# Attention probabilities turned in 32x32 squares on VectorE and weighed on four 32-row quarters of TensorE, in a layernorm, attention and low-rank feed-forward layer

## The chip, the core and the metric

The kernel runs on one core of one Trainium2 chip. The metric is device time in microseconds. A core has TensorE (PE: matmuls, with its weight loads shown apart as PEld), VectorE (DVE), ScalarE (ACT), GpSimd (POOL) and SyncE (SP, which issues most of the DMAs). SBUF has 128 partitions; a matmul result goes to one of eight PSUM banks, each of 512 floats a partition.

## The reference

All arrays are float32. `x` is 4 x 512 x 1024; there are 32 query heads, 8 key heads (so 4 query heads share a key head), and a head has 128 values.

```python
xn = layernorm(x)
qkv = xn @ w_qkv                        # 1024 x 6144
q, k, v = split(qkv)                    # 32 query heads, 8 key heads, 8 value heads
scores = einsum('bqhgd,bkhd->bhgqk', q, k) * scale
bias = -slope[h, g] * sqrt(q_pos - k_pos), and -inf where the key is later than the query
attn = softmax(scores + bias)
out = einsum('bhgqk,bkhd->bqhgd', attn, v) @ w_o
ffn = xn @ W.T + b + (one of four low-rank products, chosen for each token by a gate)
return x + out + ffn
```

## The kernel before

Three stages follow one another. `project` normalises the tokens, turns them, and multiplies them by `w_qkv`; queries, keys and values go to DRAM. `attend` computes the attention for 32 units one after another: a unit is one pair of batches `p`, one key head `h` and one batch `bi` of the pair. `finish` multiplies the heads by `w_o` and the tokens by `W` in one long product. Both big products are done in the manner of Strassen and Winograd, two levels deep: operands are summed beforehand on DVE and POOL, seven products replace eight, and the results are summed afterwards. That is why `attend` also forms sums of its results (`outer_sums`, `outer_steps`, `middle_sums`) and stores them for `finish`, on DVE and POOL beside its own work.

In `project`, an `item` is one such product. When a quarter of its result is complete, `after` (L593) has `put` (L584) store it, some steps later (`in_while`): keys and values of two heads each in one tile `t`, 128 partitions (the 128 values of a head) by 2 heads by 512 tokens (L591). The steps are numbered by `pace[2]`, and `beside` runs what has become due.

In `attend`, a tile of scores has 128 rows: 32 queries of each of four heads, so that partitions 32g to 32g+31 hold head `g` (`C` is 32, `G` is 4, `R` is 4). A unit has 16 such tiles, in four groups `i` = 3, 2, 1, 0 of four. Since a query sees no later key, tile `j` = 4i + r has only (j + 1) x 32 columns. `scores` (L1024) does one matmul for each tile (L1033), adds the distances and finds the least value on DVE (L1038), takes the exponential with its sum on ACT (L1042), and scales the rows by the inverted sum on POOL (L1047). What a tile doesn't compute in the last 128 columns of its group was cleared once (L1173).

To weigh the values, keys must lie on partitions. `transpose_probs` (L1053) turns squares of 128 by 128 on PE with an identity (L1058), four into one bank, and copies the bank to SBUF, on DVE or ACT in turn (L1061, L1063). `weigh` (L1066) then multiplies: for group `i` there are i + 1 matmuls of 512 columns, with 128 keys of the values as weights and the four heads' queries as columns (L1071), and ACT copies the bank into the result `O`, in order of heads (L1072). A unit has 40 such transposes, and ten matmuls in `weigh`. `values` (L1016) turns the unit's values on PE beforehand, four transposes and a copy, from the tile `vT`, which `load` (L984) brings with `q` and `k` two units ahead.

PE's and SP's instructions run in the order in which the code issues them (`manual_schedule`); on the other engines the tile framework orders them. The loop at L1180 mixes two units: while unit `u` is turned and weighed, the scores of the next one, `nxt`, are computed. For each `i`: `scores(nxt, i)`, then pieces of the sums (`aside`), `weigh` of a group turned two steps earlier, `transpose_probs(u, i)`. PSUM's banks are shared out by `rotation` (L1162): three for scores, three for transposes, two for results. Beside the last unit, `fill` puts in the first products of `finish`.

Of the kernel before, what the change touches and what calls it, by code (L numbers as in the profile page):

```python
# [21 lines left out]
P = 128  # L22
NH, NKV, D = 32, 8, 128
G = NH // NKV
# [41 lines left out]
def kernel(  # L66
# [55 lines left out]
    um_d = [scratch(f"um{i}", [RMAX + 1, S]) for i in range(B)]  # L122
    q_d = {(i, h): scratch(f"q{i}_{h}", [P, S // C, G, C]) for i in range(B) for h in range(NKV)}
    k_d = {(i, h): scratch(f"k{i}_{h}", [P, 2, S]) for i in range(B) for h in range(0, NKV, 2)}
    v_d = {(i, h): scratch(f"v{i}_{h}", [P, 2, S]) for i in range(B) for h in range(0, NKV, 2)}
    s_d = {i: scratch(f"s{i}", [P, 7, NP, 2, KB, HS]) for i in OUTER}
    t_d = scratch("t", [P, 4, 2, 2, 2 * KB, HS])
    m_d = {i: scratch(f"m{i}", [P, 4, 2 * KB, HS]) for i in OUTER}
# [235 lines left out]
    def project(attention):  # L364
# [5 lines left out]
        with pool("a") as sb, tc.tile_pool(name="stats", bufs=2, reuse_waits="tile") as stats:  # L370
# [182 lines left out]
            def item(st, i, acc):  # L553
# [30 lines left out]
                def put(t, row, col):  # L584
                    bi = 2 * p + row
                    if kind == "q":
                        src = t.rearrange("p a b -> p (a b)").rearrange("p (j f) -> p j f", f=2 * C)
                        dst = q_d[bi, h].rearrange("p j g k -> p j (g k)")
                        nc.sync.dma_start(out=dst[:, :, ts(col, 2 * C)], in_=src)
                    else:  # L590
                        nc.sync.dma_start(out=(k_d, v_d)[col][bi, h], in_=t)  # L591

                def after(row, col):  # L593
                    left[0] -= 1
# [365 lines left out]
    def attend(front, begin):  # L960


        early = pool("bq", side="right")
        with ExitStack() as stack:
            sb, sq = None, early.__enter__()
            units = [(p, h, bi) for p in range(NP) for h in range(NKV) for bi in range(2)]
            sizes = {"dist": (S,), "q": (S // C, G, C), "k": (S,), "vT": (S,), "bias": (S,)}
            counts = {"q": 2, "k": 2, "vT": 2, "v": 2, "pt": 10, "o": 4, "ot": 2}
            for i in (3, 2, 1, 0):
                for b in range(2):  # L970
                    sizes[f"p{i}{'xy'[b]}"] = (R, (i + 1) * P)
            sizes.update(v=(NT, D), pt=(S,), os=(3, 2, S), o=(G, S), ot=(9, HS))
            queries = ("dist", "q", "k", "vT", "bias")

            def buf(tag, name):
                where = sq if tag in queries else sb
                return where.tile([P, *sizes[tag]], F32, tag=tag, name=name, bufs=counts.get(tag, 1))

            Q, K, VT, V, PR, O, bias = {}, {}, {}, {}, {}, {}, {}

            def label(u):
                return "_".join(str(k) for k in u)
# [1 line left out]
            def load(u, queue=nc.sync):  # L984
                p, h, bi = u
                n = label(u)
                K[u] = buf("k", f"k_{n}")
                Q[u] = buf("q", f"q_{n}")
                VT[u] = buf("vT", f"vT_{n}")
                queue.dma_start(out=K[u], in_=k_d[2 * p + bi, h - h % 2][:, h % 2])  # L990
                queue.dma_start(out=Q[u], in_=q_d[2 * p + bi, h])
                queue.dma_start(out=VT[u], in_=v_d[2 * p + bi, h - h % 2][:, h % 2])

# [18 lines left out]
                bias[p, h] = t  # L1014

            def values(u):  # L1016
                n = label(u)
                V[u] = buf("v", f"v_{n}")
                tr = bank("tr", f"v_{n}")
                for t in range(NT):  # L1020
                    nc.tensor.transpose(tr[:, ts(t, P)], VT[u][:, ts(t, P)], ident)
                nc.scalar.copy(V[u], tr.rearrange("p (t d) -> p t d", d=D))

            def scores(u, i):  # L1024
                p, h, bi = u
                m = f"{label(u)}_{i}"
                tot = sb.tile([P, R], F32, tag=f"tot{i}", name=f"tot_{m}", bufs=2)
                pr = PR[u, i] = probs[i, units.index(u) % 2]
                rows = [pr[:, r, : (R * i + r + 1) * C] for r in range(R)]
                for r, row in enumerate(rows):  # L1030
                    n = (R * i + r + 1) * C
                    sc = bank("sc", f"{m}_{r}")
                    nc.tensor.matmul(  # L1033
                        sc[:, :n], Q[u][:, n // C - 1].rearrange("p g k -> p (g k)"), K[u][:, :n], start=True, stop=True
                    )

                    low = sb.tile([P, 1], F32, tag=f"low{r}", name=f"low_{m}_{r}", bufs=2)
                    nc.vector.tensor_tensor_reduce(  # L1038
                        row, sc[:, :n], bias[p, h][:, S - n :], -SCALE, BIG,
                        ALU.add, ALU.min, low,  # L1040
                    )
                    nc.scalar.activation(  # L1042
                        row, row, AF.Exp, bias=low, scale=-1.0, accum_out=tot[:, r : r + 1]
                    )
                nc.vector.reciprocal(tot, tot)  # L1045
                for r, row in enumerate(rows):
                    nc.gpsimd.tensor_scalar(  # L1047
                        row, row, tot[:, r : r + 1], 1.0, ALU.mult, ALU.mult
                    )

            PT, OS = {}, {}

            def transpose_probs(u, i):  # L1053
                for j in range(i + 1):
                    m = f"{label(u)}_{i}_{j}"
                    tr = bank("tr", m)
                    for r in range(R):
                        nc.tensor.transpose(tr[:, ts(r, P)], PR[u, i][:, r, ts(j, P)], ident)  # L1058
                    pt = buf("pt", f"pt_{m}")
                    if j % 2 == 0:  # L1060
                        nc.vector.tensor_copy(pt, tr)  # L1061
                    else:
                        nc.scalar.copy(pt, tr)  # L1063
                    PT[i, j] = pt

            def weigh(u, i):  # L1066
                if u not in O:
                    O[u] = buf("o", f"o_{label(u)}")
                po = bank("o", f"{label(u)}_{i}")
                for j in range(i + 1):  # L1070
                    nc.tensor.matmul(po, V[u][:, j, :], PT[i, j], start=(j == 0), stop=(j == i))  # L1071
                nc.scalar.copy(  # L1072
                    O[u][:, :, ts(i, P)].rearrange("p g (r k) -> p g r k", k=C),
                    po.rearrange("p (r g k) -> p g r k", r=R, k=C),
                )

            last = (NP - 1, NKV - 1)

# [80 lines left out]
            distances(units[0])  # L1159
            yield  # L1160
            sb = stack.enter_context(pool("b"))
            bank = rotation(sc=(0, 1, 2), tr=(3, 6, 7), o=(4, 5))  # L1162

            for tag in "ot os o".split():
                buf(tag, f"lay_{tag}")

            probs = {
                (i, b): buf(f"p{i}{'xy'[b]}", f"p_{i}_{b}") for i in (3, 2, 1, 0) for b in range(2)
            }
            for b in range(2):  # L1170
                for i in (3, 2, 1, 0):
                    for r in range(R - 1):
                        nc.gpsimd.memset(probs[i, b][:, r, (R * i + r + 1) * C :], 0.0)  # L1173
            for tag in "v pt".split():
                buf(tag, f"lay_{tag}")
            for i in (3, 2, 1, 0):
                scores(units[0], i)
                if i == 3:
                    values(units[0])
            for n, u in enumerate(units):  # L1180
                p, h, bi = u
                nxt = units[n + 1] if n + 1 < len(units) else None
# [3 lines left out]
                if n == len(units) - 6:  # L1186
                    front[0]()
                if not nxt:
                    early.__exit__(None, None, None)
                    front[1](O[p, h, 0])  # L1190
                    fill = begin()
                if bi == 1:
                    beside.append(middle_sums(p, h, (1, 2), "o", O[p, h, 0], True))
                for i in (3, 2, 1, 0):
                    if nxt:
                        scores(nxt, i)
                    if i > 1:
                        aside(outer, 1)
                    aside(below, 2)
                    if i < 2 or not nxt and i < 3 or n == close - 2 and i == 2:  # L1200
                        aside(beside, 2)
                    if i < 2:
                        weigh(u, i + 2)
                        if i == 0 and not nxt:
                            outer_sums(p, h, slice(HS, S))
                        next(fill, None)
                    transpose_probs(u, i)
                    next(fill, None)
                    if i == 2 and nxt:
                        values(nxt)  # L1210
                    if i == 3:
                        aside(outer, 1)
                    if not nxt:
                        if i == 3:
                            aside(beside, 2)
                        if i == 2:
                            while beside:
                                aside(beside, 1)
                        if i < 2:
                            front[3 - i]()  # L1220
                if after and after[2] == 0:
                    distances(after)
                aside(beside, 2)
                weigh(u, 1)
                next(fill, None)
                weigh(u, 0)
                if n == close:

                    while beside:
# [533 lines left out]
```

## Time and profile before

| | us |
|---|---|
| median of 3 runs | 2612.72 (2612.28 to 2616.37) |
| profiled execution, its own time | 2614.29 |
| its span, first to last instruction | 2612.5 |
| PE busy | 2559.6 (98%) |
| DVE busy | 1774.3 (68%) |
| ACT busy | 608.5 (23%) |
| POOL busy | 1911.8 (73%) |

A matmul call in float32 appears as two pairs of instructions, a weight load (LDWEIGHTS) and a MATMUL each; a transpose is one pair. The mean duration of a MATMUL is longer than its spacing in a stream of them, because they are pipelined. By the table of stages, `project` lasts to about 1110 us, the attention from there to about 1820, and `finish` from there to the end:

| stage, us | PE busy | DVE | ACT | POOL | DMA share |
|---|---|---|---|---|---|
| 0 to 1110 | 1075.7 | 792.4 | 127.7 | 883.7 | 0.78 |
| 1110 to 1770 | 655.5 | 450.3 | 434.9 | 494.1 | 0.66 |
| 1770 to 1820 | 46.3 | 31.3 | 21.3 | 20.1 | 0.73 |
| 1820 to 2612.5 | 782.1 | 500.4 | 24.7 | 513.8 | 0.82 |

In the lists of groups, a line gives the code line, the engine and its operation, the tiles and the shapes, the count, busy us and mean ns of one, and the idle time of the engine before them with what ended it.

### The profile page before, as it was taken

How to read it: one execution, taken by the hardware profiler on the slowest of the kernel's cores; microseconds unless marked ns; L12 is line 12 of the kernel's file. 1: busy time of each engine (PE TensorE's matmuls, PEld its weight loads, DVE VectorE, ACT ScalarE, POOL GpSimd, SP SyncE). 2: the span in 40 equal slices, each digit the busy share in tenths (PEclk: the TensorE clock that was granted, in tenths of full speed). 3: DMA queues.
4: the chain of work that ended last, by engine and by line, in shares of the span. 5: the costliest groups of instructions: out<-in, count | busy, mean ns of one | idle time of the engine just before them, and what ended most of it. 6: DMA issues, size and time to landing. Idle time of an engine off the chain costs nothing.

```text
span 2612.5 us, 36400 instructions
## 1 busy us (share of the span) xinstructions
PE 2559.6 (98%) x11872; PEld 2062.2 (79%) x11872; DVE 1774.3 (68%) x3654; ACT 608.5 (23%) x1682; POOL 1911.8 (73%) x2038
## 2 busy tenths in 40 slices
PE   7999999999999999999999999999999999999999
PEld 6888888788788888866666666666788888888887
DVE  7786777877676667566767676676765666656584
ACT  3011111100000000176666666663000000000000
POOL 4687888877798889767777777684865666756593
PEclk9999999999999999999999999999999999999999
DMA  4499998969977878446767676767997878878884
GB/s 145 126 272 323 286 330 241 290 190 323 283 252 216 257 215 266 124 125 200 241 203 240 206 237 207 252 209 255 356 315 267 308 298 306 306 272 310 307 331 159
DMA packets 509455, 656.23 MB, mean 251 GB/s; under 512 B 153514, under 2 KB 422186, under 8 KB 499155
## 3 DMA queue, kind: packets, MB, share of 16 engines
q1 hardware_dynamic: 437202, 566.47, 65.3%
q10 hardware_dynamic: 70752, 82.85, 9.6%
q0 software_dynamic: 1312, 4.59, 0.5%
q8 instruction: 95, 1.56, 0.2%
q14 instruction: 94, 0.76, 0.1%
HBM read 392.72 MB, written 261.10 MB: 250 GB/s over the span
## 4 chain that ended last, share of the span: by engine, by line
PE 68%; DVE 3%; DMA 3%; POOL 2%; issue 1%; SPq 0%; ACT 0%; DVEq 0%; POOLq 0%; ACTq 0%
PE pc L1342 15%; PE po L1071 10%; PE psc L1033 9%; PE pd L1342 8%; PE pc_q L568 6%; PE pa L1342 4%; PE ptr L1058 4%; PE pc_kv L568 3%; PE pd_q L568 3%; PE pd_kv L568 2%; PE pa_q L568 1%; POOL ti_q L139 1%; DVE p L1038 1%; DVE pt L1061 1%; DMA sa<-s 1%; PE pa_kv L568 1%
## 5 line engine op out<-in xcount | busy, mean ns | idle before, releaser
L1047 POOL TENSOR_SCALAR p<-p,tot 128x416 f32<-128x416 f32 (+15 forms) x512 | 298.9, 603 | 119.4 <-DVE tot L1045 111.1
L1071 PE MATMUL po<-pt,v 128*128 128x512 f32 x640 | 290.9, 593 | 1.7 <-DVE pt L1061 1.7
L139 POOL TENSOR_TENSOR t<-w 128x640 f32<-128x640 f32 x95 | 186.8, 1967 | 133.5 <-DMA w<-m 55.2
L1038 DVE CUSTOM_DVE_ANT_0 p<-psc,bias 128x416 f32<-128x416 f32 (+15 forms) x512 | 224.8, 441 | 80.9 <-PE psc L1033 57.3
L1042 ACT ACTIVATE p<-p,low 128x416 f32<-128x416 f32 (+15 forms) x512 | 263.0, 515 | 54.1 <-DVE low L1038 37.1
L1033 PE MATMUL psc<-k,q 128*128 128x416 f32 (+15 forms) x1024 | 272.1, 407 | 3.5 <-DVE low L1038 3.0
L1033 PEld LDWEIGHTS psc<-k,q 128*128 128x128 f32 x1024 | 166.1, 190 | 75.4 <-issue 45.2
L139 POOL TENSOR_TENSOR t<-w,t 128x640 f32<-128x640 f32 x95 | 196.0, 2063 | 34.8 <-PE pc L1342 31.0
L1071 PEld LDWEIGHTS po<-pt,v 128*128 128x128 f32 x640 | 116.7, 190 | 110.8 <-issue 98.8
L139 POOL TENSOR_TENSOR wr<-wr 128x256 f32<-128x256 f32 x220 | 173.2, 789 | 41.3 <-DMA wr<-in_w_o_dram 12.7
L1058 PEld LDWEIGHTS ptr<-ident,p 128*128 128x128 f32 x1280 | 147.2, 141 | 70.0 <-issue 38.3
L1061 DVE COPY pt<-ptr 128x512 f32<-128x512 f32 x192 | 131.3, 684 | 81.6 <-PE ptr L1058 81.2
L568 PE MATMUL pc_q<-xi,ti_q 128*128 128x256 f32 x640 | 166.7, 383 | 4.0 <-DVE q L136 2.7
L1058 PE MATMUL ptr<-ident,p 128*128 128x128 f32 x1280 | 167.6, 274 | 2.9 <-DVE pt L1061 0.4
L139 DVE TENSOR_TENSOR wr<-wr 128x256 f32<-128x256 f32 x220 | 140.4, 638 | 10.3 <-DMA wr<-t 5.7
L139 POOL TENSOR_TENSOR ti_q<-w_q 128x256 f32<-128x256 f32 x128 | 105.9, 827 | 52.5 <-PE pc_kv L568 29.9
L178 ACT COPY m<-pc 128x256 f32<-128x256 f32 x30 | 11.2, 372 | 560.4 <-PE pc L1342 549.6
L568 PEld LDWEIGHTS pc_q<-xi,ti_q 128*128 128x128 f32 x640 | 120.1, 191 | 26.5 <-issue 8.3
L568 PE MATMUL pd_q<-xi,ti_q 128*128 128x256 f32 x448 | 116.2, 382 | 7.0 <-POOL ti_q L139 7.0
L1072 ACT COPY o<-po 128x512 f32<-128x512 f32 x128 | 75.2, 587 | 175.0 <-PE po L1071 175.0
L1342 PE MATMUL pc<-sa,w 128*128 128x256 f32 x480 | 112.4, 381 | 3.5 <-DMA sa<-s 3.5
L1342 PE MATMUL pd<-s,t 128*128 128x256 f32 x480 | 112.3, 381 | 0.0
(345 smaller groups left out, 5929.2 us busy)
## 6 DMA issues: line engine op xcount, KB each, us to landing
sa<-s SPq DMA_DIRECT2D x98, 640.0 KB, 8.3
s<-ot SPq DMA_DIRECT2D x107, 384.0 KB, 4.8
m<-wr SPq DMA_DIRECT2D x70, 512.0 KB, 5.7
w<-m SPq DMA_DIRECT2D x28, 1280.0 KB, 7.6
w_q<-in_w_qkv_dram SPq DMA_DIRECT2D x16, 2048.0 KB, 12.3
q<-q SPq DMA_DIRECT2D x32, 1024.0 KB, 7.2
s<-os SPq DMA_DIRECT2D x45, 512.0 KB, 4.7
t<-wr SPq DMA_DIRECT2D x40, 512.0 KB, 4.2
```

What stands on the lines that cost most here:

```text
L139: return eng.tensor_tensor(dst, u, v, ALU.subtract)
L178: nc.scalar.copy(dst, alike(src, dst))
L568: nc.tensor.matmul(dst, ops_w[m][:, c, :], XI[i][m][:, c, :], start=start and c == 0, stop=c == 1, skip_group_check=True,)
L1033: nc.tensor.matmul(sc[:, :n], Q[u][:, n // C - 1].rearrange("p g k -> p (g k)"), K[u][:, :n], start=True, stop=True)
L1038: nc.vector.tensor_tensor_reduce(row, sc[:, :n], bias[p, h][:, S - n :], -SCALE, BIG, ALU.add, ALU.min, low,)
L1042: nc.scalar.activation(row, row, AF.Exp, bias=low, scale=-1.0, accum_out=tot[:, r : r + 1])
L1047: nc.gpsimd.tensor_scalar(row, row, tot[:, r : r + 1], 1.0, ALU.mult, ALU.mult)
L1058: nc.tensor.transpose(tr[:, ts(r, P)], PR[u, i][:, r, ts(j, P)], ident)
L1061: nc.vector.tensor_copy(pt, tr)
L1071: nc.tensor.matmul(po, V[u][:, j, :], PT[i, j], start=(j == 0), stop=(j == i))
L1072: nc.scalar.copy(O[u][:, :, ts(i, P)].rearrange("p g (r k) -> p g r k", k=C), po.rearrange("p (r g k) -> p g r k", r=R, k=C),)
L1342: nc.tensor.matmul(bk, w[:, k], x[:, k], start=start and k == 0, stop=stop and k == KB - 1, skip_group_check=True,)
```

## The change

The values are now turned in `project`: before a tile of values is stored, PE transposes its eight squares (four for each of the two heads), ACT copies them back over the tile, and SP stores it by rows of tokens, four steps later. `attend` no longer turns values. It loads them four times, once into each quarter of 32 partitions, so that each quarter `g` holds the values of all 512 keys: 16 blocks of 32 keys, one after another along the free dimension.

The probabilities are no longer turned on PE. `turn` has DVE transpose each tile in squares of 32 by 32, where each square stays in its quarter of partitions: afterwards partitions 32g to 32g+31 hold 32 keys of a block, and the columns are the queries of head `g`. That is one or two DVE instructions a tile, 24 a unit. `weigh` multiplies block by block: for each of 16 blocks of 32 keys and each of four heads one matmul, of 32 rows on the quarter `g` of PE (`tile_position`), over the queries that see the block (512 - 32b columns). A head's result gathers in its own PSUM bank over the whole unit, and `settle` has ACT copy the four banks at its end. Banks are now four for scores and four for results. The probabilities have one buffer for a group instead of two, and their turned form has two, one for each batch. `weigh` for unit `u` takes blocks 0 and 1 beside the scores of group 3, then 2 to 4, 5 to 8, and 9 to 15; `turn(nxt, i)` follows one step behind `scores(nxt, i)`.

```diff
@@ put
-                        nc.sync.dma_start(out=(k_d, v_d)[col][bi, h], in_=t)
+                        for j in range(2):
+                            tr = bank("tr", f"v_{n}_{j}")
+                            for c in range(NT):
+                                nc.tensor.transpose(tr[:, ts(c, P)], t[:, j, ts(c, P)], ident)
+                            nc.scalar.copy(t[:, j], tr)
+                        dst = v_d[bi, h].rearrange("(c k) j d -> k j c d", k=P)
+                        src = t.rearrange("p j (c d) -> p j c d", d=D)
+                        in_while(4, lambda: [
+                            nc.sync.dma_start(out=dst[:, j], in_=src[:, j]) for j in range(2)
+                        ])
...
@@ attend
             def values(u):
...
+                src = v_d[2 * p + bi, h - h % 2].rearrange("(b k) j d -> k j b d", k=C)[:, h % 2]
+                for g in range(G):
+                    nc.sync.dma_start(out=V[u][ts(g, C)], in_=src)
...
-            def transpose_probs(u, i):
...
+            def turn(u, i):
...
+                for r in range(R):
+                    j = R * i + r
+                    for part in range(2):
+                        b, e = 8 * part, min(j + 1, 8 * part + 8)
+                        if b < e:
+                            nc.vector.transpose(
+                                PT[u][part][:, : e - b, ts(j - b, C)], pr[:, r, b * C : e * C]
+                            )
+
+            PARTS = {3: range(0, 2), 2: range(2, 5), 1: range(5, 9), 0: range(9, S // C)}
...
+            def weigh(u, blocks, lo=0, hi=S):
+                for b in blocks:
+                    at = slice(max(lo, b * C), hi)
...
+                    for g in range(G):
+                        if (u, g) not in PO:
+                            PO[u, g] = bank("o", f"{label(u)}_{g}")
+                        nc.tensor.matmul(
+                            PO[u, g][:, at], V[u][ts(g, C), b, :], probs_of(u, g, b, at),
+                            start=b == 0, stop=(b + 1) * C == hi, skip_group_check=True,
+                            tile_position=(g * C, 0),
+                        )
+
+            def settle(u, at=slice(0, S)):
...
+                for g in range(G):
+                    nc.scalar.copy(O[u][:, g, at], PO[u, g][:, at])
...
-            bank = rotation(sc=(0, 1, 2), tr=(3, 6, 7), o=(4, 5))
+            bank = rotation(sc=(0, 1, 2, 3), o=(4, 5, 6, 7))
...
                     if nxt:
                         scores(nxt, i)
+                        if i < 3:
+                            turn(nxt, i + 1)
+                        else:
+                            values(nxt)
...
-                    if i < 2:
-                        weigh(u, i + 2)
...
-                    transpose_probs(u, i)
...
-                    if i == 2 and nxt:
-                        values(nxt)
+                    if nxt:
+                        weigh(u, PARTS[i])
+                        if i == 0:
+                            turn(nxt, 0)
+                    elif i > 1:
+                        weigh(u, range(8 * (3 - i), 8 * (4 - i)), HS)
+                    elif i == 1:
+                        settle(u, slice(HS, S))
+                        weigh(u, range(8), 0, HS)
+                        outer_sums(p, h, slice(HS, S))
...
-                weigh(u, 1)
-                next(fill, None)
-                weigh(u, 0)
+                settle(u, slice(0, S if nxt else HS))
```

## The prediction

> **What bounds the kernel now.** I read the page's busy shares first, then the table by stage, then the chain of waits inside one unit of attention, and last the groups by shape in that stage. First the page: TensorE (PE) is busy in every slice at the full granted clock, so the end moves only where PE's own stream gets longer or shorter, or is made to wait.
>
> ```profile
> PE 2559.6 (98%) x11872; PEld 2062.2 (79%) x11872; DVE 1774.3 (68%) x3654; ACT 608.5 (23%) x1682; POOL 1911.8 (73%) x2038
> PE   7999999999999999999999999999999999999999
> PEclk9999999999999999999999999999999999999999
> ```
>
> The table by stage, for the attention (columns: span, busy us and count of PE, PEld, DVE, ACT, POOL, then clock, DMA share, GB/s):
>
> ```profile
> 1135.00:1770.00 635.00, 631.16 (x2808) 398.76 (x2807) 432.76 (x1341) 415.00 (x1213) 474.12 (x580) 1.00 0.66 216
> ```
>
> A unit (one batch, one key head, four query heads) makes 20 instructions on `po`, and this window holds 588 of them, so 29.3 units: 21.7 us each, of which PE 21.6, POOL 16.2, DVE 14.8, ACT 14.2, DMA two thirds. The chain through one unit (start, us, what) shows that nearly all of it is PE's own work:
>
> ```profile
> 1397.47 0.88 PE ptr L1058 x8
> 1398.35 1.03 PE psc L1033 x8
> 1399.38 2.58 PE po L1071 x6
> ...
> 1404.97 3.13 PE psc L1033 x8
> 1408.10 0.02 issue
> 1408.12 0.69 DVE p L1038
> 1408.82 0.01 DVE low L1038
> 1408.82 0.61 DVE pt L1061
> 1409.44 0.04 issue
> 1409.48 0.66 PE ptr L1058 x4
> ...
> 1420.04 0.94 PE psc L1033 x8
> ```
>
> From it I take PE's paces. A 512-column `po` instruction: 2.58/6 = 0.43 us, or 0.835 ns a column. A 128-column transpose: 0.88/8 = 0.11. The last eight scores have 32 to 128 columns and still take 0.94/8 = 0.117 each: each PE instruction brings its own weight load, and below some 140 columns that pair is the price, however few the columns. One matmul call is two such instructions (`psc`: 512 calls, x1024). From 1398.35 to 1420.04 the unit adds up: scores 7.8 us, `po` 8.6, transposes of probabilities and values 3.9, and 1.4 in which PE waits behind DVE.
>
> ```profile
> L1071 PE MATMUL po<-pt,v 128*128 128x512 f32 x588 | 267.2, 593 | 0.8 <-DVE pt L1061 0.8
> L1061 DVE COPY pt<-ptr 128x512 f32<-128x512 f32 x175 | 119.6, 684 | 76.4 <-PE ptr L1058 76.2
> L1038 DVE CUSTOM_DVE_ANT_0 p<-psc,bias 128x512 f32<-128x512 f32 x29 | 20.1, 692 | 5.6 <-PE psc L1033 5.2 <-PE ptr L1058 0.4
> L1038 DVE CUSTOM_DVE_ANT_0 p<-psc,bias 128x32 f32<-128x32 f32 x30 | 5.6, 186 | 0.3 <-PE psc L1033 0.3
> L1072 ACT COPY o<-po 128x512 f32<-128x512 f32 x117 | 68.7, 587 | 155.6 <-PE po L1071 155.6
> ```
>
> **What leaves PE.** In attention all of `po`, the transposes and the wait between them: 8.6 + 3.9 + 1.4 = 13.9 us a unit. Only the scores' 7.8 stay.
>
> **What comes.** Per unit 16 blocks of 32 keys times 4 heads: 64 calls, 128 instructions and 128 weight loads, where `po` had 20. A call streams 512, 480, ... 32 columns; over the 16 blocks that is 4352 columns for one head. No row shows two PE instructions side by side, so I bound it from both ends.
> - No overlap at all. Twelve blocks of 160 to 512 columns (4032 in sum): 8 x 4032 x 0.835 ns = 26.9 us; four small ones 4 x 8 x 0.117 = 3.7. Together 30.7 us.
> - All four quarters abreast, loads free: 2 x 4352 x 0.835 ns = 7.3 us.
> - What I take lies between. The two instructions of a call use the same quarter, so the second must follow the first; in the trace PE starts its matmuls in program order. Then only the second of one head can run beside the first of the next: one `columns x 0.835 ns` per head instead of two. Loads I take at the only pace shown, one after another at 0.117 a pair. Eight blocks of 288 to 512 columns (3200): 4 x 3200 x 0.835 = 10.7 us; eight of 256 and fewer are held by the loads: 8 x 8 x 0.117 = 7.5. Together 18.2 us. If loads of different quarters also overlap, 4 x 4032 x 0.835 + 4 x 4 x 0.117 = 15.3.
>
> The Trainium skill, "TensorE: Matmul & The Clock Gate", section "LDWEIGHTS (loading the stationary operand)", speaks against the change: a load's time goes by its columns, so one of 32 rows costs what one of 128 costs. By its formula the 128 loads are an estimate of 128 x 107 ns = 13.7 us, more than all four quarters abreast would stream. The same page's "Part 3: Packing small matmuls" speaks for it: 3.07 times the speed for four row quarters; by that an estimate of 30.7/3.07 = 10 us. It also says that matmuls keep program order. No run here shows either yet.
>
> **Sum for a unit.** 7.8 + 18.2 = 26.0 us against 21.7: 4.3 longer, times 32 units = 138 us.
>
> **Other engines.** DVE loses six copies (119.6/29.3 = 4.1 us) and gains 24 turns over 4352 columns a lane. No row shows a turn. The nearest line on DVE goes from 186 ns at 32 columns to 692 at 512, 1.05 ns a column and 152 fixed: 4.6 + 3.6 = 8.2 us; at least 4.6 if the starts are hidden, perhaps 12.8 at twice the pace per column. DVE then has 18.9 us (15.3 to 23.5) in 26: hidden behind PE; in a unit of 20 it would be the bound. ACT loses four copies and the value copy, about 2.9 us. POOL keeps its 16.2. SP loads the values four times, 1 MB in 512-byte rows for 0.25 MB; the trace's packets of 512 bytes take 28 ns, so 2048 x 28/16 = 3.6 us of 16 engines, less 0.7 for the old ones: DMA from 66% to some 70% of a longer unit. The four issues are asked a whole unit ahead of their use, so I cost them at nothing; queued behind them on SP are the stores of the sums, 0.3 to 1.0 us each to issue now, which nothing reads before the next stage. If that cover went, the 7.2 us in which 1 MB of `q` lands would show once a unit.
>
> **New waits.** The output banks are now held for a whole unit. After the last `weigh`, ACT copies four banks, 4 x 0.587 = 2.35 us, while PE does the four longest scores, 3.1 us: covered by 0.75; behind these copies on ACT wait the next exponentials. A turn waits on DVE for POOL's scaling, and behind it wait the reductions that free the score banks; POOL has its 16.2 of 26 and the turn stands one step after its scores, so I take nothing, at worst the 1.4 us of wait that is there today. PE goes between full array and quarters eight times a unit; if each time it must run empty, that is the 593 - 428 = 165 ns by which an instruction outlasts its pace: 1.3 us a unit. Today's changes of line show none, so I take zero and keep 42 us (32 x 1.3) for the range.
>
> **The values' turn moves.** 128 transposes go from attention, where they are counted as gone, into the projection before it, which is PE's as well: 128 x 0.11 = 14 us. They wait for sums asked for three to fourteen steps earlier, so no stall; ACT there has time for 32 copies. The 24 clears on POOL at the start (2.2 us) go, beside PE's work: nothing.
>
> **Sum.** The profiled execution took 2614.3 us (span 2612.5). 2614.3 + 138 + 14 = 2766; the median of the runs is 1.6 lower, so 2765. This case's own range: 15.3 instead of 18.2 gives 7.8 + 15.3 - 21.7 = 1.4 a unit, 45 + 14, so 2672; with all changes of mode run empty 2807, and with 1 us of new waits a unit 2839.
>
> **Rivals.**
> - Faster: four abreast, and loads of different quarters overlap as well. PE needs 7.8 + 7.3 = 15.1; then DVE's 18.9 decides: (18.9 - 21.7) x 32 = -90, + 14: 2537. For it: the quarters share neither rows nor banks. Against: program order, and 128 loads. It decides as soon as the weighing takes under 13.9 - 14/32 = 13.5 us a unit.
> - Four abreast, loads in single file: 128 x 0.117 = 15.0, so 1.1 longer a unit, 2614 + 35 + 14 - 2 = 2661; at the transposes' 0.11 (14.1) 2633. About no change is the edge of this one.
> - The quarters don't run beside one another, so the change doesn't do what it says: 30.7 + 7.8 - 21.7 = 16.8 a unit, 538 + 14, so 3165. For it: no row shows any overlap of matmuls.
>
> **How the numbers follow.** Pairwise overlap 0.48; faster 0.20; four abreast with loads in file 0.13; no overlap 0.15; 0.04 for waits between 2840 and 3165. The likeliest gives 2765 (own range 2670 to 2840). To leave out no more than 2 in 10 the range drops only the last two: 2530 to 2840. What this measurement can tell from no change is 0.2%, 5 us: faster 0.20, same 0.03 out of the file case, slower 0.77.
>
> **What would show it.** Right: attention units of 25 to 26 us, PE still busy throughout, the `po` instructions of one call about 0.43 us apart at 512 columns with the next head's first starting with the second, and 0.117 apart in the small blocks; DVE near 19 us a unit. Wrong: all four heads starting within one 0.43 us, a unit under 20 us with DVE or POOL in the chain (the faster rival), or a unit near 38 (no overlap); wrong too, if the chain shows DVE turns waiting for POOL, or the value loads.

## The result, and the profile after

The changed kernel takes 2777.1 us (median of 3 runs, 2777.04 to 2781.39) against 2612.72: 1.063 times as long (95% interval 1.0606 to 1.0654). The profiled execution took 2777.04, its span 2775.3. By stages, from the start of the first 512-column score: it begins at 1125.9 us of the span instead of 1115.9 (the values' turn in the projection: +10.0); from there to the start of the last `po` 856.2 instead of 700.9 (+155.3); from there to the end 793.1 instead of 795.7 (-2.6). So the attention makes the loss, 26.9 us a unit instead of 21.7. (Here and below, a unit's time is the mean from one 512-column score to the next, over units 4 to 28 of 32.)

The page's busy shares and two of its lines by slice, of the kernel after:

```profile
PE 2532.5 (91%) x14112; PEld 2050.6 (74%) x14112; DVE 1868.9 (67%) x4230; ACT 515.9 (19%) x1558; POOL 1862.3 (67%) x2014
...
PE   7999999999999999877776877777899999999999
...
PEclk9999999999999999988988889898999999999999
```

PE is no longer busy throughout: in the attention it is idle a quarter of the time, and there, and only there, its granted clock falls. The table by stage (the columns are those of before):

```profile
1200.00:1900.00 700.00, 530.99 (x4162) 330.52 (x4162) 467.51 (x1667) 279.36 (x950) 390.48 (x521) 0.89 0.78 213
```

A unit is now 32 instructions of scores and 128 of weighing, so this window holds 4162/160 = 26.0 units: of each unit's 26.9 us PE is busy 20.4, DVE 18.0, POOL 15.0, ACT 10.7. No engine is full. The chain of waits through a part of one unit (start, us, what) shows why:

```profile
1516.69 2.32 POOL os L139
1519.01 2.51 POOL p L1058 x4
...
1522.78 2.35 ACT p L1053 x8
...
1525.15 0.19 DVE tot L1056
...
1525.43 0.52 POOL p L1058
...
1525.97 2.24 DVE pt L1075 x8
1528.21 0.21 DVE p L1049
...
1528.53 1.93 ACT p L1053 x8
```

PE isn't in it. A long sum on POOL (`os`) holds up the scaling of four tiles; and then the engines take turns: exponentials on ACT, the inverse of the sums on DVE, scaling on POOL, the turn of those same tiles on DVE (L1075), and only behind it DVE's reduction of the next group's scores (L1049), which the next exponentials need. The waits of the window 1200 to 1900 (total us, times, longest):

```profile
ACT p L1053 <- DVE low L1049: 322.8, 91, 5.1
POOL p L1058 <- DVE tot L1056: 299.8, 91, 6.2
PEld psc L1044 <- DVE low L1049: 235.8, 197, 7.7
PE psc L1044 <- DVE low L1049: 166.2, 78, 7.1
...
DVE pt L1075 <- POOL p L1058: 105.0, 104, 6.4
```

DVE stands in a turn that waits for POOL 104 times, four times a unit, 4.0 us a unit; PE stands 166.2 us, 6.4 a unit, before a score whose bank DVE has not yet freed, since the reduction that frees it is queued behind that turn. In the code `turn` of a group is issued one step after its scores, and so behind the next group's reductions. But only PE and SP follow the code there: the tile framework put each turn on DVE directly behind its own group's inverse.

### The profile page after: what moved, and what is told of

The parts are those of the page before. It is cut to its first block, busy times and chain, and to the rows that moved or that the text cites. A ratio compares the mean times of both kernels' runs of the same rounds, so it can differ in the third digit from the quotient of the medians.

```text
span 2775.3 us, 40663 instructions
## 1 busy us (share of the span) xinstructions
PE 2532.5 (91%) x14112; PEld 2050.6 (74%) x14112; DVE 1868.9 (67%) x4230; ACT 515.9 (19%) x1558; POOL 1862.3 (67%) x2014
## 4 chain that ended last, share of the span: by engine, by line
PE 43%; POOL 12%; DVE 9%; ACT 7%; DMA 4%; issue 3%; SPq 2%; ACTq 0%; POOLq 0%; DVEq 0%
PE pc L1370 14%; PE pd L1370 7%; ACT p L1053 6%; PE pc_q L568 6%; POOL p L1058 4%; DVE pt L1075 4%; PE pa L1370 4%; PE pd_q L568 3%; PE pc_kv L568 3%; POOL os L139 2%; DMA s<-os 2%; PE pd_kv L568 1%; PE pa_q L568 1%; POOL o L139 1%; POOL os L136 1%
## 5 line engine op out<-in xcount | busy, mean ns | idle before, releaser
L1044 PE MATMUL psc<-k,q 128*128 128x416 f32 (+15 forms) x1024 | 338.7, 480 | 196.5 <-DVE low L1049 195.9
L1058 POOL TENSOR_SCALAR p<-p,tot 128x416 f32<-128x416 f32 (+15 forms) x512 | 243.6, 495 | 374.9 <-DVE tot L1056 374.9
L1044 PEld LDWEIGHTS psc<-k,q 128*128 128x128 f32 x1024 | 192.8, 221 | 327.6 <-DVE low L1049 274.6
L1095 PE MATMUL po<-pt,v 32*128 32x256 f32 (+15 forms) x4160 | 327.3, 445 | 6.5 <-ACT o L1105 3.7
L1075 DVE STREAM_TRANSPOSE pt<-p 128x256 f32<-128x256 f32 (+7 forms) x768 | 241.4, 353 | 133.9 <-POOL p L1058 122.5
L1095 PEld LDWEIGHTS po<-pt,v 32*128 32x128 f32 x4160 | 221.9, 214 | 117.1 <-issue 67.6
L1049 DVE CUSTOM_DVE_ANT_0 p<-psc,bias 128x416 f32<-128x416 f32 (+15 forms) x512 | 193.4, 431 | 4.4 <-PE psc L1044 3.0
L568 PEld LDWEIGHTS pc_q<-xi,ti_q 128*128 128x128 f32 x640 | 119.8, 190 | 23.2 <-issue 6.5
L1056 DVE RECIPROCAL tot<-tot 128x4 f32<-128x4 f32 x128 | 22.7, 177 | 139.0 <-ACT p L1053 139.0
L1370 PE MATMUL pd<-s,w 128*128 128x256 f32 x480 | 111.5, 379 | 0.7 <-DVE s L139 0.7
L1370 PE MATMUL pc<-s,t 128*128 128x256 f32 x480 | 111.4, 379 | 0.0
```

The costliest lines, as they stand in the source:

```text
L568: nc.tensor.matmul(dst, ops_w[m][:, c, :], XI[i][m][:, c, :], start=start and c == 0, stop=c == 1, skip_group_check=True,)
L1044: nc.tensor.matmul(sc[:, :n], Q[u][:, n // C - 1].rearrange("p g k -> p (g k)"), K[u][:, :n], start=True, stop=True)
L1049: nc.vector.tensor_tensor_reduce(row, sc[:, :n], bias[p, h][:, S - n :], -SCALE, BIG, ALU.add, ALU.min, low,)
L1058: nc.gpsimd.tensor_scalar(row, row, tot[:, r : r + 1], 1.0, ALU.mult, ALU.mult)
L1075: nc.vector.transpose(PT[u][part][:, : e - b, ts(j - b, C)], pr[:, r, b * C : e * C])
L1095: nc.tensor.matmul(PO[u, g][:, at], V[u][ts(g, C), b, :], probs_of(u, g, b, at), start=b == 0, stop=(b + 1) * C == hi, skip_group_check=Tr ...
```

## What had to be told apart

Two things could make 26.9 us. **PE's own work** could take 26.0, as predicted: neighbouring quarters overlap pairwise and the loads run in file. Or PE needs far less, and the **order on DVE and POOL** makes the unit. The runs come in five groups. The first two ask about these theories; the rest follow what remained.

## Experiment 1: all blocks of one head, then the next (head_major)

```diff
-                for b in blocks:
...
-                    for g in range(G):
+                for g in range(G):
+                    for b in blocks:
```

The same matmuls in an order in which neighbours in the program mostly share a quarter.

> Within each part of weigh the loop over heads is put outside the loop over blocks, so that calls in succession use the same quarter of PE. Theory A (quarters overlap because neighbouring calls use different quarters, four abreast): the overlap goes, weighing takes about 27 to 31 us a unit instead of about 7.5, PE becomes the bound with 35 to 38 us a unit against 26.9 now, so about 3030 to 3150 us. Theory B (PE takes calls out of order by itself, or the short time per block has another cause): within 1% of 2777.

Measured: 3149.8 us (one run), 37.5 us a unit, at the upper end of what theory A gave. PE's stretches in one unit (timeline: start, us, line, the first instruction's tile and shape, how many instructions):

```profile
1500.22 12.49 PE L1095 MATMUL po<-pt,v 32*128 32x224 f32 x56
...
1518.98 1.97 PE L1095 MATMUL po<-pt,v 32*128 32x512 f32 x16
...
1523.34 4.94 PE L1095 MATMUL po<-pt,v 32*128 32x448 f32 x24
...
1529.82 6.03 PE L1095 MATMUL po<-pt,v 32*128 32x352 f32 x32
```

Interleaved by heads, the same four stretches take 2.07, 1.95, 2.38 and 2.33 us (sums_spread, in the next section). With two blocks to a head, four instructions in a row on one quarter, nothing is lost: 1.97. With three blocks the time doubles, with four it is 2.6 times as long, and with seven six times. The clock belongs into this reading. The table by windows (clock in the third column from the end):

```profile
1500.30:1512.60 12.30, 12.30 (x56) 12.07 (x56) 3.40 (x16) 3.25 (x11) 1.25 (x4) 0.50 0.85 288
...
1519.00:1523.30 4.30, 4.30 (x25) 2.20 (x24) 0.88 (x3) 0.84 (x3) 4.22 (x3) 1.00 0.03 4
```

The seven-block stretch ran at half clock; at full clock it would be some 6.2 us by estimate (half of 12.49), or 0.11 a pair, about the price in file. So quarters do run beside one another, as if PE looked ahead a few instructions for one that can start, and whether heads overlap depends on their order. In the changed kernel the order is the good one; how good, the quick units of experiment 4 show.

## Experiments 2 to 4: DVE in the code's order (order_pinned, divide_later, sums_spread)

```diff
+            in_order = tc.manual_schedule(engines={DVE})
+            in_order.__enter__()
...
```

order_pinned holds DVE to the order of the code around the loop, so that `turn` stands behind the next group's reductions.

> DVE keeps the order of the code in the attention: turn(nxt, i + 1) behind the reductions and the reciprocal of scores(nxt, i), where the changed kernel has each turn directly behind the reciprocal of its own group, ahead of the next group's reductions. Theory O (each turn waits on DVE for POOL's scaling, and the next reductions wait behind it, so that ACT, POOL, DVE and PE take turns instead of working side by side): the wait of the turn goes except behind POOL's long sums, the reciprocal's wait of some 1.1 us for ACT stays four times a unit; 24 to 25 us a unit instead of 26.9, so 2685 to 2715 us. Rival D (DVE's own work with the turns in it is the bound, or it is slowed by POOL): within 1% of 2777. Rival P (weighing on PE is the bound): within 1% of 2777.

Measured: 2694.7 us (one run), 24.1 a unit, as theory O gave: 82 us of the loss came with DVE's order. The edit fixes that order for all of DVE's steps, the sums too; the chain above points at the turn's place in it. divide_later also issues the inverse and POOL's scaling of a group one step later (`divide(u, i)`, behind the turn before it), so that DVE doesn't wait for the exponentials just asked for.

> As order_pinned, and the reciprocal and POOL's scaling of group i are issued behind turn(nxt, i + 1), so that DVE does not wait for ACT either. Theory O: another 4 us a unit less, about 20 to 21 us a unit, 2570 to 2600 us. Rivals D and P: within 1% of 2777.

Measured: 2675.59 (one run), 23.3 a unit. That is a smaller gain than expected (2570 to 2600): every second unit takes 18.9, the other 27.3. In the window 1200 to 1800 DVE still waits for POOL, in fewer and longer pieces:

```profile
DVE pt L1081 <- POOL p L1064: 137.9, 50, 9.5
```

POOL does four long sums of results (`outer_sums`, about 2.4 us each) in a row after every second unit, and the scaling stands behind them. sums_spread issues them one at a time between the scalings, and drops a pause of three steps before DVE's second set of sums:

```diff
-                    if n + 1 == close:
+                    if nxt:
...
-                        outer.append(outer_steps(p, h))
+                        outer.append(outer_steps(p, h, nc.vector if n + 1 == close else nc.gpsimd))
```

> As divide_later, and the four sums of 2.4 us each that POOL does in a row after every second unit are issued one by one between its scalings. Theory O with POOL's block as the last wait: about 18.5 to 19.5 us a unit, with DVE's 18 us of work as the bound, 2510 to 2550 us, below both kernels. Rival D: within 1% of 2777. If O holds but the block is hidden already: within 1% of divide_later.

Measured: 2646.73 (2642.74 to 2652.26), ratio 1.0125 (1.0102 to 1.0148), well short of the 2510 to 2550 expected. Every second unit now takes 17.0 us, the other still 27.4. The quick one shows PE's real price. The timeline of PE; the first line is the end of a stall, in brackets the idle time before it:

```profile
1428.60 5.76 PE L1044 MATMUL psc<-k,q 128*128 128x416 f32 x8 [5.63 <-DVE low L1049]
1434.29 1.95 PE L1101 MATMUL po<-pt,v 32*128 32x512 f32 x16
1436.17 2.53 PE L1044 MATMUL psc<-k,q 128*128 128x288 f32 x8
1438.63 2.38 PE L1101 MATMUL po<-pt,v 32*128 32x448 f32 x24
1440.93 1.67 PE L1044 MATMUL psc<-k,q 128*128 128x160 f32 x8
1442.54 2.33 PE L1101 MATMUL po<-pt,v 32*128 32x352 f32 x32
1444.80 1.16 PE L1044 MATMUL psc<-k,q 128*128 128x32 f32 x8
1445.88 2.07 PE L1101 MATMUL po<-pt,v 32*128 32x224 f32 x56
```

From start to start, weighing takes 1.88 + 2.30 + 2.26 + 2.0 = 8.4 us a unit, not 18.2. All four quarters abreast would be 7.3. The 24 instructions of the second `po` line stream 2 x 4 x 1248 columns, 8.3 us in file at 0.835 ns; they take 2.30, 3.6 times as quick, where pairs of heads alone would give 4.2 at best. And 32 pairs in 2.26 are 0.07 a pair, below the 0.117 at which a pair goes in the whole array: loads for different quarters overlap too. Single starts in the trace agree: four begin 7 ns apart, then four more of the same width one pass later (349 ns at 416 columns), although the program asks for both instructions of a head before the next head. (The trace doesn't name the quarter; that each of the four is another head's is read from this pattern.) The scores cost a little more than before, 8.5 instead of 7.8: at each change between whole array and quarters the next instruction starts some 0.1 us later than the columns ask, 0.2 around a group of scores (the second group takes 2.46 instead of 2.26). PE needs 16.9 to 17.0 us a unit.

The first line holds one more thing: eight scores that take 3.38 us in the next unit take 5.76 here, behind a stall of 5.63. The clock granted in that stretch is 0.57.

## Experiments 5 to 7: what POOL's scaling, its sums and the values cost (no_scaling, sums_balanced, values_only)

no_scaling is the changed kernel without POOL's scaling of the rows, so its probabilities aren't divided by their sums; the order on DVE is the framework's.

```diff
-                    nc.gpsimd.tensor_scalar(
-                        row, row, tot[:, r : r + 1], 1.0, ALU.mult, ALU.mult
-                    )
```

> The changed kernel with POOL's scaling of the probabilities left out (so the rows keep their sums), everything else as it is: the turns wait on ACT's exponentials alone. Theory O: each group's chain loses POOL's part (0.6 us to the first scaled row, and the stall behind POOL's long sums), 2.5 to 4 us a unit of 26.9, so 2650 to 2700 us. Rival D: within 1% of 2777.

Measured: 2605.18 us (one run), 20.7 a unit. The time falls by 172 us, 5.4 for each of 32 units, more than expected, and comes out a little under the kernel before. Units 2 to 6 take 16.9 us each, which is PE's own need; later ones, up to unit 28, vary from 16.9 to 26.8, so other waits are left. The edit takes 243.6/32 = 7.6 us a unit of work off POOL, too, and this run doesn't separate the two. But POOL was not full (15.0 of 26.9), which speaks for the wait: nothing between exponentials and turn stands behind POOL any more.

sums_balanced gives the long sums and the sums for the stores fixed places, one a group, in the two units after a pair (`aside(outer, 1)` at every `i`; `pause(3)` in the lists `beside` and `below`).

> As sums_spread, but POOL's four long sums go one to each group of the unit after a pair, its four sums for the stores to the unit after that, and DVE's sums wait for them (one to each group, the pause before the second set back in). Theory O: sums_spread ran one unit in 17.0 us and the next in 27.4, because DVE's sums and turns stood behind POOL's; with that gone both come to 18 to 20 us, 22.4 to about 18.8 in the mean, so 2515 to 2560 us, below the kernel before. Rival D (DVE, POOL and ACT together have no more to give; a stall only moves): 2630 us or more.

Measured: 2709.88, ratio 1.037 (1.0355 to 1.0386), worse than sums_spread and far from the 2515 to 2560 expected: units of 31.9 and 17.0. In the window 1200 to 1800 DVE waits 87.9 us, up to 8.0 at a time, for one of the two buffers that all store sums share (`ot`), which SP is still storing. The likely reason is that sums spread out in time hold their buffers longer.

values_only makes the values' part of the change alone in the kernel before: turned in the projection, loaded by rows (once, into 128 partitions).

> The kernel before with one part of the change alone: values turned in the projection, stored by rows and loaded once into 128 partitions; probabilities are turned and weighed as before. By the prediction's sum: 128 transposes of 0.11 us, 14 us more in the projection, and about as much less in the attention (0.61 us a unit, 19.5 us at most): 2605 to 2620 us. Rival (the stores or the banks in the projection make PE wait, so that this part costs more than its transposes): 2630 us or more.

Measured: 2617.33 (2612.88 to 2620.92), ratio 1.0013 (1.0003 to 1.0022), as expected. The first score begins 11 us later, and a unit takes 21.5 instead of 21.7: the step costs nearly what it gives.

## Experiments 8 and 9: own buffers for the sums (balanced_room, spread_pause)

```diff
-                m = buf("ot", f"ot_{n}")[:, : (3 + kept) * g]
+                m = buf({1: "oa", 7: "ob", 5: "ot"}[which[0]], f"ot_{n}")[:, : (3 + kept) * g]
```

balanced_room is sums_balanced with a buffer for each kind of store sum (the room comes from rows of probabilities stored without gaps) and one long sum on POOL a step earlier; spread_pause is sums_spread with these buffers and the pause.

> As sums_balanced, but the three kinds of sums for the stores each have a buffer of their own (room comes from storing only the columns of a probability row that are used), and POOL's third long sum goes one step earlier. In sums_balanced DVE stood 88 us of a 600 us window, some 7 to 8 us a pair of units, before a sum whose buffer was still being stored. Theory W (the order is right, that buffer wait is what is left): units of 17 and 32 us become 17.5 and 20.5, 24.2 to about 19 in the mean, 2530 to 2570 us. Rival D (no slack left on DVE, POOL and ACT): 2640 us or more.

> As sums_spread, with the pause before DVE's second set of sums set back in and the buffers of balanced_room; POOL's sums all in the unit after a pair. Theory W: DVE's sums no longer stand before POOL's last long sum, but the turns still wait for POOL in that unit: 27.4 us becomes 21 to 24, the other stays near 17 to 18, 2545 to 2600 us. Rival D: 2640 us or more.

Measured: 2630.38, ratio 1.0053 (1.0041 to 1.0066), units of 23.0 and 19.6; and 2677.4, ratio 1.0241 (1.0227 to 1.0256). With the buffers and the earlier sum, balanced_room takes 79.5 us less than sums_balanced. Both runs missed what theory W gave (2530 to 2570 and 2545 to 2600). In both, DVE's turn still waits for POOL: 81.4 and 138.0 us in the window 1140 to 1750.

## Experiments 10 to 12: part of the scaling on ACT, and the value loads (act_scales_half, values_in_rows, no_value_loads)

act_scales_half is balanced_room with groups 1 and 0 scaled on ACT, which is least busy, and with one of DVE's sums moved into the wait for the first exponentials:

```diff
+                    if i < 2:
+                        nc.scalar.activation(row, row, AF.Identity, scale=tot[:, r : r + 1])
+                        continue
```

> As balanced_room, and the probabilities of groups 1 and 0 are scaled on ACT instead of POOL (8 of 16 rows a unit, some 3 us), and DVE does one of its sums while it would wait for ACT's first exponentials. In balanced_room the stall that is left is in the unit with POOL's long sums: the scalings stand behind them, the last turn behind the scaling, and the first weighing behind the turn (3.7 us). Theory O: with ACT's idle time used for that, POOL has some 15 us and 10 us of work in the two units, both units come to 17.5 to 19.5 us, 2500 to 2560 us, below the kernel before. Rival D (DVE is full, 18 us a unit and what its operations lose to POOL): no better than 2600 us.

Measured: 2605.25 (2595.06 to 2613.75), ratio 0.9962 (0.9949 to 0.9975): quicker than the kernel before, by some 8 to 10 us, with all of the work done. It is not the 2500 to 2560 expected; the rival's "no better than 2600" is what came. Units take 23.3 and 17.8. The wait of the turn for POOL is down to 31.4 us in the same window.

values_in_rows lays the values out in DRAM so that a partition is read in one run of 8 KB instead of 512-byte pieces, and issues the loads at the start of a unit.

```diff
-                src = v_d[2 * p + bi, h - h % 2].rearrange("(b k) j d -> k j b d", k=C)[:, h % 2]
+                src = v_d[2 * p + bi, h - h % 2][:, h % 2]
...
```

> As act_scales_half, but the values lie in DRAM as a quarter reads them: for each of 32 partitions 16 blocks of 128 values in a row, 8 KB at a time, so that the four loads of a unit are 128 runs of 8 KB instead of 2048 of 512 bytes; they are issued at the start of a unit, ahead of the stores of the sums. Theory V (in act_scales_half the four loads, 1.1 us each to issue on SP behind stores that wait, with DMA busy 0.96, come late and stall PE, which then runs on a lower clock): DMA's share falls, units of 23.3 and 17.8 us become 17.5 to 19.5 both, 20.4 to about 18.5 in the mean, 2520 to 2575 us. Rival D (DVE, POOL and ACT set the pace): within 1% of 2605.

Measured: 2617.7 (2607.43 to 2628.64), ratio 1.0021 (1.0007 to 1.0035). The attention gains 26.3 us: from the first 512-column score to the last `po` it takes 654.2 instead of 680.5. But that first score begins at 1150.6 instead of 1124.7 us, and the gain is gone. The values now leave the projection in 128 small stores on SP instead of 32; in the projection PE waits 16.0 us for POOL's sums of weights (`ti_q`) where it waited 5.5, and why isn't shown. no_value_loads has every unit but the first two use the first two's values:

```diff
+                if u not in units[:2]:
+                    V[u] = V[units[bi]]
+                    return
```

> act_scales_half, with the value loads of all units but the first two left out: the later units weigh the values of the first two. Theory V (the four loads of a unit, the prediction's cost of nothing, are what keeps act_scales_half at 20.4 us a unit where PE's own work is 15 to 17): DMA's share falls from 0.96 to 0.75 or less, about 17.5 to 18.5 us a unit, 2605 less 60 to 95 us, 2510 to 2545 us. Rival D (DVE, POOL and ACT set the pace; the loads are covered): 2590 to 2610 us.

Measured: 2580.38 (2577.99 to 2584.79), ratio 0.9873 (0.9857 to 0.989). So the four loads cost about 25 us in act_scales_half, less than half of what theory V gave. More than half of the 25 is one unit near the end, the 29th: 37.4 us in act_scales_half and 23.2 here. PE waits there for a load, 11.9 us in one piece, and 20.5 us at half clock follow. From the waits of act_scales_half in the window 1140 to 1750:

```profile
PE po L1108 <- DMA v<-v: 12.7, 4, 11.9
```

values_in_rows has no such unit, and its attention, 654.2 us, is as short as the 653.5 without any loads: in long runs and issued earlier they cost the attention nothing that shows. These loads without the delay in the projection weren't run.

The rest is not theirs: units still take 22.1 and 17.9. The longer unit shows where, first in the timeline of ACT and PE around its start, then in that of PE alone:

```profile
1515.06 0.71 ACT L1025 ACTIVATE bias<-dist,slope 128x512 f32<-128x512 f32 x1
...
1516.68 2.01 ACT L1121 COPY o<-po 128x512 f32<-128x512 f32 x4
```

```profile
1512.41 3.38 PE L1051 MATMUL psc<-k,q 128*128 128x416 f32 x8
1517.30 4.92 PE L1111 MATMUL po<-pt,v 32*128 32x512 f32 x16 [1.50 <-ACT o L1121]
1522.15 4.32 PE L1051 MATMUL psc<-k,q 128*128 128x288 f32 x8
1526.40 2.38 PE L1111 MATMUL po<-pt,v 32*128 32x448 f32 x24
```

Once in two units ACT computes a `bias` and scales group 0 before `settle` copies the output banks, and PE, done with its longest scores, waits 1.50 us for the first bank, and then for the other three as ACT copies them one after another. So the 16 weighings take 4.92 us instead of 1.95; behind the waits the clock granted from 1519 to 1525 is 0.50, and eight scores take 4.32 instead of 2.53. In the records a spell at half clock lasts a whole multiple of 3.41 us (but for one cut off by the end of the run), here two of them, 6.83 us, of which half is lost. Of the 13 such units from the fifth on, nine have this spell and take 23.2 us; four have the wait (1.2 to 1.5 us) without it and take 19.6 to 19.9. So a long unit adds up from PE's own 17.0, some 2.9 of waits for the banks, and 3.4 of clock where the spell comes. The units between take 17.7 to 18.3.

## Why the prediction was right in the number and wrong in the reasons

2765 us was predicted, in the likeliest case, and 2777.1 came, a unit of 26.0 us predicted against 26.9. That the number fits is luck: two large errors cancel. Weighing took 9.8 us less than its term, the scores 0.7 more, and waits that were put at nothing took 9.9.

- **The failed step on PE: "The two instructions of a call use the same quarter, so the second must follow the first; in the trace PE starts its matmuls in program order. Then only the second of one head can run beside the first of the next", and "Loads I take at the only pace shown, one after another at 0.117 a pair".** All the rows of before were of whole-array instructions, and program order on one resource was read as a rule for four. The term 18.2 us measured 8.4: 9.8 us a unit too much, 314 us over 32 units. The first rival (four abreast, loads overlapping) was right about PE: it gave 15.1 a unit, and PE needs 17.0. The 3.07 times of the Trainium skill, "TensorE: Matmul & The Clock Gate", "Part 3: Packing small matmuls", erred less than the row: its estimate of 10 us stands beside 8.4 measured. Its rule that matmuls keep program order isn't seen here across quarters, and the estimate of 13.7 us for loads in file isn't either; the measurement decides.
- **The failed step on the waits: the turn behind POOL's scaling, "so I take nothing, at worst the 1.4 us".** All waits together cost 9.9 us a unit (26.9 - 17.0): PE is idle 169 of the window's 700 us, 6.5 a unit, and at a mean clock of 0.89 up to 3.0 more are lost to half pace. Without the scaling that the turn waits for (no_scaling) 5.4 a unit are gone, with DVE in the code's order (order_pinned) 2.6. What is left of the 9.9 isn't divided up by any run. That it is waits and not work, act_scales_half shows: it does all of the work in 171.9 us less than the changed kernel, by order, buffers and the place of a part of the scaling. The argument that the turn "stands one step after its scores" is one about the code; the order on DVE is the framework's, and it was another. The prediction itself had named "DVE turns waiting for POOL" as the sign of its being wrong.
- **DVE's load** was right: turns of 8.2 us a unit predicted, 241.4/32 = 7.5 measured, 1.04 ns a column and 158 fixed (from 32 to 224 columns); DVE 18.9 predicted, 18.0 measured. But the faster rival's step "then DVE's 18.9 decides" failed as well: DVE is busy 81% at most (no_scaling, 405.6 of the 500 us from 1200 to 1700), and the waits between engines decide first.

The price of a turn, from the groups by shape of the kernel after:

```profile
L1075 DVE STREAM_TRANSPOSE pt<-p 128x256 f32<-128x256 f32 x260 | 112.7, 441 | 81.5 <-POOL p L1058 80.4
L1075 DVE STREAM_TRANSPOSE pt<-p 128x224 f32<-128x224 f32 x52 | 20.3, 391 | 1.2
...
L1075 DVE STREAM_TRANSPOSE pt<-p 128x32 f32<-128x32 f32 x52 | 9.9, 191 | 10.9 <-POOL p L1058 10.9
```

- **The value loads, costed at nothing.** In the changed kernel the 512-byte packets take 49 ns, not 28, so 2048 x 49/16 = 6.3 us of 16 engines a unit instead of 3.6. The 28 were read from packets in the first 400 us of the kernel before; its attention has none of 512 bytes. In the changed kernel no wait of PE for a load shows; in act_scales_half the loads cost about 25 us, most of it in one late load.
- **The change of mode, taken as zero,** costs PE some 0.7 us a unit (scores of 8.5 instead of 7.8); the 1.3 kept for the range held it.
- **settle, "covered by 0.75":** true while ACT has nothing ahead of it. In the versions that scale on ACT the cover is gone in every second unit.
- **The values' turn:** +14 predicted, +10.0 measured; alone, with what it gives back, +3.
- **No overlap (3165):** head_major, at 3149.8 and 37.5 us a unit against 38.5, ends close to it, but by other terms: its weighing stretches sum to 25.4 us, some of it at half clock, and its scores to 12.7.
- **A slip:** by its own row the prediction's 29.3 units are 588/20 = 29.4, which moves its figures for a unit by under 0.1 us.

**What stays open.** Why the clock falls where it does: in the kernel before, 1.4 us of waiting a unit leave it at 1.00; in no_value_loads 1.5 us in one piece are followed by 6.83 us at half in nine units and by none in four; in head_major it falls with PE busy throughout. No run varied this alone. The account of no_value_loads' longer units is read from one trace, and a version with `settle` ahead of the `bias` on ACT wasn't run. Eight of the twelve runs came out slower than the theories that they were to test gave. The rival, that DVE, POOL and ACT together have little more to give, isn't refuted by them, though none of these engines is full. And one of DVE's sums (`ot<-o`, 512 columns) takes 2.67 us in the changed kernel and 0.69 before; it runs beside the first of POOL's long sums in the stretch that was read, and whether POOL slows it was not varied.

## What to carry to other kernels

Price small matmuls on quarters of the array by the order in which they are issued: with neighbours on different quarters they ran 3.6 times as quick as in file, with six or more in a row on one quarter much of that was lost. When a step moves from PE to an engine whose order a framework decides, look up (or fix) where it will stand in that queue and what it waits for before taking a wait as hidden: the move here freed 4.7 us of PE a unit and lost 9.9 in waits, more than half of them in a chain through three engines. And count a stall of PE at more than its length where the granted clock falls behind it.

## What the runs showed of the hardware

- Float32 matmuls on four 32-row quarters start 7 ns apart, and their loads overlap too (0.07 us a pair against 0.117). This holds against the program's order: in full with four instructions in a row on one quarter, only in part with six (1.97 us against 1.95 for 16 instructions; 4.94 against 2.38 for 24).
- The clock granted to PE drops to one half in spells of whole multiples of 3.41 us, behind stalls as short as 1.5 us (no_value_loads, nine units of 13), and without any stall in head_major (20.5 of 37.5 us a unit). The Trainium skill, "TensorE: Matmul & The Clock Gate", "Part 1: The HAM clock gate (the "warmup" mystery)", gives a window of 3413 ns, which the spells match, and a fall after at least one idle window; the falls behind 1.5 us and behind none go beyond that rule.
- 512-byte packets took 28 ns in the first 400 us of the kernel before, at a DMA share of 0.76, and 27 in values_only's attention (0.68), where a unit's values go once into 128 partitions. Where they go four times into 32 they took 49 in the changed kernel's attention (0.78) and 50 in act_scales_half's (0.96). So the share doesn't explain the difference; what does wasn't varied.
